# First attention of a Perceiver kernel: the projections of a superblock spread evenly over its four steps, and two evictions together in every second step

## The chip, the cores and the metric

The kernel runs on one core of a Trainium2 chip. A core has five engines that work at the same time and wait for each other by semaphores: TensorE (PE, matrix products into the accumulator memory PSUM; its weight loads are shown apart, as PEld), VectorE (DVE), ScalarE (ACT), GpSimd (POOL) and the queue that issues most transfers (SP). The metric is the time of one execution in microseconds on the device; lower is better. Of the unchanged kernel three runs are at hand: 1592.82, 1596.47 and 1597.17 us, median 1596.47.

## The reference, cut to what matters

Six sublayers are applied to one sequence x of 128 rows of 256. The change touches the first one, an attention of the 128 rows over 12544 context rows of 192, with 16 heads of 16:

```python
q = (x @ Wq + bq).reshape(B, N, NUM_HEADS, HEAD_DIM)
k = (y @ Wk + bk).reshape(B, M, NUM_HEADS, HEAD_DIM)
v = (y @ Wv + bv).reshape(B, M, NUM_HEADS, HEAD_DIM)
scores = jnp.einsum('bnhd,bmhd->bhnm', q, k) * scale
attn = jax.nn.softmax(scores, axis=-1)
out = jnp.einsum('bhnm,bmhd->bnhd', attn, v).reshape(B, N, IMAGE_DIM)
h = jax.nn.relu(out @ W1 + b1)
return h @ W2 + b2
```

Here x is layer-normalised and y is the context. Everything is float32. Behind it come a causal self-attention of the 128 rows, a dense mixture of eight experts, a second attention over the same context with 16 heads of 64, a small self-attention and a second mixture.

## The kernel before, in words

The first attention treats the 16 heads as two octets, j = 0 and 1. For each octet the 12544 context rows are walked in 13 superblocks of up to 1024 rows (`SB`), and each superblock in groups of 256 rows: four per superblock, one in the last, short superblock. That makes 49 groups per octet and 98 in all; `groups[t]` holds (superblock m, group g). The main loop over t (line 562) does one step per group, and all instructions are issued in the order in which the loop writes them (`tc.manual_schedule`), so each engine works off its own list in order.

In step t, TensorE computes the scores of group t (`scores`, line 421: 16 recorded matmuls of 256 columns) into two PSUM tiles st[0] and st[1] of two banks each. `keep` (line 434) lets ScalarE copy st[0] and then st[1] to SBUF slots (line 441), while VectorE takes a running maximum of st[1] and then of st[0] (line 447). The two engines never read one of the two tiles at the same time: the copy of st[1] waits for its maximum, and the maximum of st[0] waits for its copy. The two tiles are the only ones for scores, so the scores of the next group need both emptied.

A range is ten groups (nine in the last of an octet). The softmax of a range is shifted by its own maximum. When a range has ended, in the next step, VectorE folds the running maximum (`fold`, line 455, instructions of line 464, or of line 462 in a range of nine), TensorE transposes it, VectorE reduces it to one value per head and row (`range_maximum`, line 466), one or two steps later TensorE spreads the value over columns (`range_spread`, line 480) and ScalarE copies the spread to SBUF (line 494). Then the scores of that range, which lie in their slots, are shifted: by POOL for three quarters and by VectorE for one quarter (`shift`, line 502, instructions of line 506), 12 and 11 groups behind the scores (`LAG` = 13; VectorE one step ahead of POOL). ScalarE takes the exponents in place (line 517), and one step later TensorE multiplies them with the values (`attend`, line 519, 32 recorded matmuls, "p * v"). At the end of a range the result is collected and turned (`collected`, `gather`, lines 538 and 543).

Keys and values are projected four groups ahead (`AHEAD` = 4) by `pieces(t + 4)`, line 368. A projection of 192 context columns has two parts per half superblock r: a tiled part over the last 64 columns, in which both halves run at the same time on two halves of the array, and a whole part over the first 128, one per half (`project_keys`, line 200; `project_values`, line 216). One unit, the keys or the values of a superblock, fills two PSUM banks, one per half, and each bank is evicted by one instruction: keys with the bias (line 390), values into their place among columns of ones (line 256). In the first steps, up to t = 11, ScalarE does these evictions (`filling`), from then on VectorE. Before the change the four steps of a superblock do this (g is the group projected for): g = 0 tiled keys, whole keys of half 0, its eviction; g = 1 whole keys of half 1, its eviction; g = 2 and g = 3 the same for values. So g = 0 and g = 2 are heavy steps of TensorE and g = 1 and g = 3 light ones. The short superblock does all of it in one step.

PSUM has eight banks: four for the two score tiles, two for the projections (`ps_w`, taken in turn, and used by `range_maximum`, `range_spread` and `gather` too), one "m" for a range's spread and one "o" for p * v. The order of a step for VectorE is: maximum of st[1], maximum of st[0], a fold if a range has ended, the shift, the eviction. For TensorE: scores, a spread if one is due, the projection, p * v, then a range's maximum and the turning of a result. Where the value buffer that is to be filled is the one that p * v still reads (`same`, line 591), the projection is issued behind p * v.

## Time and profile before

| what | us |
|---|---|
| three runs | 1592.82, 1596.47, 1597.17 |
| profiled execution, its own time | 1592.66 |
| its span, first to last instruction | 1590.9 |
| PE busy in the span | 1507.9 |
| DVE busy | 1169.4 |
| ACT busy | 996.3 |
| POOL busy | 851.1 |
| first scores of the first attention start | 13.86 |
| POOL's first shift starts | 57.70 |
| last p * v of the first attention starts | 459.7 |

The first attention is thus the first 29% of the span. In the profile, a row of the timeline holds a start time, a length, the engine, the line of the program, the operation, the tiles (written <- read), their shapes and a count; rows of equal instructions that follow each other are merged into one. In brackets stands how long the engine was idle before it and what ended that. [...] Starts of consecutive instructions on one engine tell more than their lengths, since an instruction's length holds the acknowledgement of its writes, which overlaps the next one.

### The profile page before, as it was taken

How to read it: one execution, taken by the hardware profiler on the slowest of the kernel's cores; microseconds unless marked ns; L12 is line 12 of the kernel's file. 1: busy time of each engine (PE TensorE's matmuls, PEld its weight loads, DVE VectorE, ACT ScalarE, POOL GpSimd, SP SyncE). 2: the span in 40 equal slices, each digit the busy share in tenths (PEclk: the TensorE clock that was granted, in tenths of full speed). 3: DMA queues.
4: the chain of work that ended last, by engine and by line, in shares of the span. 5: the costliest groups of instructions: out<-in, count | busy, mean ns of one | idle time of the engine just before them, and what ended most of it. 6: DMA issues, size and time to landing. Idle time of an engine off the chain costs nothing.

```text
span 1590.9 us, 39751 instructions
## 1 busy us (share of the span) xinstructions
PE 1507.9 (95%) x17130; PEld 1156.8 (73%) x17130; DVE 1169.4 (74%) x1238; ACT 996.3 (63%) x1221; POOL 851.1 (54%) x559
## 2 busy tenths in 40 slices
PE   7999989999789998999999999999999999999978
PEld 4566666666545877877778787787787777777868
DVE  4798978999863327677777777777777777778952
ACT  5898979889853225665655665565665655655531
POOL 0588877888820000863863864864764764761000
PEclk9999999999997999999999999999999999999979
DMA  3211112111193661322222222232232222225930
GB/s 104 61 41 42 46 42 61 41 42 46 47 270 129 238 167 25 98 84 83 83 80 86 81 81 86 80 93 74 87 94 80 87 81 86 81 81 153 306 135 4
DMA packets 68737, 146.62 MB, mean 92 GB/s; under 512 B 8905, under 2 KB 27089, under 8 KB 68562
## 3 DMA queue, kind: packets, MB, share of 16 engines
q1 hardware_dynamic: 68258, 143.30, 30.0%
q8 instruction: 135, 2.21, 0.6%
q10 hardware_dynamic: 304, 0.79, 0.2%
q14 instruction: 40, 0.33, 0.1%
HBM read 143.92 MB, written 0.13 MB: 91 GB/s over the span
## 4 chain that ended last, share of the span: by engine, by line
PE 62%; DVE 6%; ACT 2%; POOL 1%; DMA 1%; issue 1%; SPq 0%; DVEq 0%; ACTq 0%
PE x_s L958 11%; PE x_v L234 10%; PE x_o L1043 10%; PE x_k L212 9%; PE x_v L227 5%; PE x_k L209 4%; PE f_h L1249 2%; PE f_h L824 2%; PE k L212 2%; PE f_py L841 2%; DVE x_part L1066 1%; POOL x_p L506 1%; PE k L209 1%; DVE x_folded L1005 1%; PE f_py L1258 1%
## 5 line engine op out<-in xcount | busy, mean ns | idle before, releaser
L1024 POOL TENSOR_TENSOR x_p<-x_p,x_spread 128x1024 f32<-128x1024 f32 (+1 forms) x175 | 402.6, 2324 | 165.1 <-ACT x_spread L1017 164.9
L506 POOL TENSOR_TENSOR x_p<-x_p,x_spread 128x512 f32<-128x512 f32 (+1 forms) x184 | 325.6, 1820 | 121.0 <-ACT x_spread L494 61.1
L1066 DVE TENSOR_REDUCE x_part<-x_p 128x256 f32<-128x1024 f32 (+1 forms) x175 | 329.4, 1923 | 1.6 <-ACT x_p L1032 1.6
L975 ACT COPY x_p<-x_s 128x1024 f32<-128x1024 f32 (+1 forms) x200 | 198.0, 996 | 177.7 <-DVE x_mx L982 97.9
L982 DVE TENSOR_TENSOR x_mx<-x_s,x_mx 128x1024 f32<-128x1024 f32 (+1 forms) x161 | 193.4, 1201 | 127.1 <-PE x_s L958 118.7
L1071 POOL TENSOR_TENSOR x_sums<-x_sums,x_part 128x256 f32<-128x256 f32 x161 | 118.7, 738 | 303.4 <-DVE x_part L1066 303.1
L441 ACT COPY x_p<-x_s 128x1024 f32<-128x1024 f32 x196 | 193.4, 1016 | 48.5 <-PE x_s L428 33.2
L234 PEld LDWEIGHTS x_v<-ywv_lo,x_ctx_lo 128*128 128x128 f32 x1568 | 189.3, 192 | 38.3 <-issue 36.8
L1032 ACT ACTIVATE x_p<-x_p 128x1024 f32<-128x1024 f32 (+1 forms) x200 | 197.8, 1037 | 1.4 <-DVE x_p L1024 1.3
L517 ACT ACTIVATE x_p<-x_p 128x1024 f32<-128x1024 f32 x196 | 196.3, 1062 | 0.2 <-DVE x_p L506 0.2
L1043 PE MATMUL x_o<-x_p,x_v 128*64 128x128 f32 x3136 | 193.6, 276 | 0.4
L234 PE MATMUL x_v<-ywv_lo,x_ctx_lo 128*128 128x128 f32 x1568 | 193.1, 276 | 0.0
L447 DVE TENSOR_TENSOR x_mx<-x_s,x_mx 128x1024 f32<-128x1024 f32 x140 | 168.2, 1221 | 32.1 <-PE x_s L428 17.2
L1043 PEld LDWEIGHTS x_o<-x_p,x_v 128*64 128x64 f32 x3136 | 169.6, 137 | 12.3 <-issue 1.5
L958 PE MATMUL x_s<-x_qT,x_kT 64*128 64x128 f32 x2744 | 177.7, 279 | 0.0
L212 PE MATMUL x_k<-x_ctx_lo,ywk_lo 128*128 128x512 f32 (+1 forms) x364 | 171.6, 594 | 0.0
L958 PEld LDWEIGHTS x_s<-x_qT,x_kT 64*128 64x128 f32 x2744 | 160.2, 188 | 15.6 <-issue 15.4
L943 ACT COPY x_v<-x_v 128x512 f32<-128x512 f32 (+1 forms) x208 | 116.2, 563 | 79.3 <-PE x_v L234 78.8
L227 PEld LDWEIGHTS x_v<-ywv_hi,x_ctx_hi 64*128 64x128 f32 x1568 | 106.8, 188 | 48.4 <-issue 25.1
L428 PE MATMUL x_s<-x_qz,x_kT 32*128 32x256 f32 x1568 | 117.6, 401 | 17.7 <-ACT x_p L441 16.6
L530 PE MATMUL x_o<-x_p,x_v 128*32 128x128 f32 x3136 | 111.7, 276 | 10.0 <-ACT x_p L517 8.5
L530 PEld LDWEIGHTS x_o<-x_p,x_v 128*32 128x32 f32 x3136 | 81.9, 109 | 53.9 <-ACT x_p L517 18.9
(257 smaller groups left out, 1761.1 us busy)
## 6 DMA issues: line engine op xcount, KB each, us to landing
x_ctx_lo<-in_ctxT_dram SPq DMA_DIRECT2D x119, 512.0 KB, 4.0
x_ctx_hi<-in_ctxT_dram SPq DMA_DIRECT2D x238, 128.0 KB, 3.8
f_w<-in_L_ffn_W_dram SPq DMA_DIRECT2D x32, 512.0 KB, 4.9
k_lo<-in_ctxT_dram SPq DMA_DIRECT2D x12, 512.0 KB, 10.0
f_gating<-n_kernel_gating_EDF_dram SPq DMA_DIRECT2D x8, 512.0 KB, 6.9
f_up<-L_ffn_kernel_up_EDF_dram SPq DMA_DIRECT2D x8, 512.0 KB, 7.5
f_wd<-ffn_kernel_down_EFD_dram SPq DMA_DIRECT2D x8, 512.0 KB, 7.3
k_hi<-in_ctxT_dram SPq DMA_DIRECT2D x24, 128.0 KB, 7.9
```

What stands on the lines that cost most here:

```text
L212: nc.tensor.matmul(ps[r][:, :h], wk[0][:, js], lo[:, r * h : (r + 1) * h], start=False, stop=True)
L234: nc.tensor.matmul(ps[r][:, kc * P : (kc + 1) * P], lo[:, r * h + kc * P : r * h + (kc + 1) * P], wv[0][:, js], start=False, stop=True, sk ...
L441: nc.scalar.copy(ps[t][k], st[k].rearrange("p a n -> p (a n)"))
L506: engine.tensor_tensor(v, v, by[:, banks].unsqueeze(2).to_broadcast([P, n, 2, 256]), ALU.add)
L517: nc.scalar.activation(ps[t][k], ps[t][k], AF.Exp)
L530: nc.tensor.matmul(os[b][32 * i : 32 * i + 32, u * P : (u + 1) * P], v[:, 2 * g + c, 17 * (2 * i + u) : 17 * (2 * i + u) + 32], p[i // 2][ ...
L958: nc.tensor.matmul(st[:, u, c * P : (c + 1) * P], kTs[t][rs, ks], qT[rs, j, :], start=True, stop=True)
L975: nc.scalar.copy(scores_kept(ps[t][i], sts[i].shape[2] // P), sts[i])
L1024: engine.tensor_tensor(v, v, spreads[j].unsqueeze(2).to_broadcast([P, 2, n, P]), ALU.add)
L1032: nc.scalar.activation(v, v, AF.Exp)
L1043: nc.tensor.matmul(o[us, 0:P], vs[t][:, c0 + c, us], p[:, n0 : n0 + P], start=(c0 + c == 0), stop=(c0 + c == total - 1), skip_group_check= ...
L1066: nc.vector.tensor_reduce(part, v, AX.X, ALU.add)
```

## The change

Three things change, all in the first attention.

First, the projection of a unit is cut so that each of its two steps has the same number of matmuls: the even step (g = 0 or 2) does the tiled part and the first half of the whole part of half 0; the odd step (g = 1 or 3) does the second half of it, evicts bank 0, does the whole part of half 1 and evicts bank 1. For keys this cuts each 512-column matmul into two of 256 columns (`of=2`). Both banks stay taken from the even step to the end of the odd one. Where another use of these two banks falls into the even step (`shared`: a range has just ended, a result is turned, or a spread is due in the next step), the pair of steps keeps the old division. The short superblock stays in one step.

Second, in an odd step the projection with its evictions is issued ahead of VectorE's shift (`evicting`); in an even step the shift stays ahead.

Third, the first steps are cut accordingly: the keys of the first superblock start before the loop with the tiled part and all of the whole part of half 0, in two halves, and the rest follows in step 0. The test `same` now looks at the last group alone (and the short superblock), since the values of an unfinished unit are written in the last step.

```diff
--- before.py
+++ after.py
@@ -197,23 +197,32 @@
             )
         return lo, hi, h
 
-    def project_keys(name, wk, cx, j, bank=None):
+    def project_keys(name, wk, cx, j, bank=None, of=1):
 
         lo, hi, h = cx
         ps = [(bank or ps_w)(f"{name}_{r}") for r in range(2)]
         js = slice(j * P, (j + 1) * P)
 
         def tiled():
-            for r in range(2):
-                rs = slice(64 * r, 64 * r + 64)
-                nc.tensor.matmul(ps[r][:, :h], wk[1][rs, js], hi[rs, :h], start=True, stop=False)
-
-        def whole(r):
-            nc.tensor.matmul(ps[r][:, :h], wk[0][:, js], lo[:, r * h : (r + 1) * h], start=False, stop=True)
+            for i in range(of):
+                n = slice(i * h // of, (i + 1) * h // of)
+                for r in range(2):
+                    rs = slice(64 * r, 64 * r + 64)
+                    nc.tensor.matmul(
+                        ps[r][:, n], wk[1][rs, js], hi[rs, n], start=(i == 0), stop=False, skip_group_check=True
+                    )
+
+        def whole(r, parts=range(of)):
+            for i in parts:
+                n = h // of
+                nc.tensor.matmul(
+                    ps[r][:, i * n : (i + 1) * n], wk[0][:, js], lo[:, r * h + i * n : r * h + (i + 1) * n],
+                    start=False, stop=True, skip_group_check=True,
+                )
 
         return ps, tiled, whole
 
-    def project_values(name, wv, cx, j, bank=None):
+    def project_values(name, wv, cx, j, bank=None, of=1):
 
         lo, hi, h = cx
         ps = [(bank or ps_w)(f"{name}_{r}") for r in range(2)]
@@ -229,8 +238,9 @@
                         skip_group_check=True,
                     )
 
-        def whole(r):
-            for kc in range(h // P):
+        def whole(r, parts=range(of)):
+            n = h // P // of
+            for kc in range(parts.start * n, parts.stop * n):
                 nc.tensor.matmul(
                     ps[r][:, kc * P : (kc + 1) * P], lo[:, r * h + kc * P : r * h + (kc + 1) * P],
                     wv[0][:, js], start=False, stop=True, skip_group_check=True,
@@ -361,9 +371,16 @@
 
                 return bank_o(name) if name.endswith("_1") else bank_m(name)
 
+
+            spread_at = {max(l + 2, l0 + LAG - 2): b for b, (l0, l) in enumerate(zip(start_of, last_of))}
+
+            def shared(t):
+
+                return t > 0 and (last[t - 1] or (t > LAG and last[t - LAG - 1]) or t + 1 in spread_at)
+
             def behind(t):
 
-                return ((1, 2), (3, 4), (5, 6), (7,))[t] if t < 4 else (t + AHEAD,)
+                return ((2,), (3, 4), (5, 6), (7,))[t] if t < 4 else (t + AHEAD,)
 
             def pieces(t):
 
@@ -377,8 +394,6 @@
                 lo, hi, h = ctxs[m]
                 v = vs[m % NV]
                 bias = cols[:, COL_BK + j : COL_BK + j + 1]
-                work_of = {"k": ([], [], []), "v": ([], [], [])}
-
 
                 filling = t < LAG - 1 + AHEAD
 
@@ -394,29 +409,38 @@
                     dst = v[:, r * n : (r + 1) * n, 0:136].rearrange("p k (h d) -> p k h d", d=17)[:, :, :, 0:16]
                     evacuated(filling, dst, src[:, :h].rearrange("p (k h d) -> p k h d", h=8, d=16))
 
-                def first_half(kind, make, w, evacuate):
+                def unit(kind):
+                    if kind == "k":
+                        make, w, out = project_keys, xwk, keys_out
+                    else:
+                        make, w, out = project_values, xwv, values_out
                     bank = spare if kind == "v" and m < 2 else None
-                    unit = make(f"x0_{kind}{m}", w, ctxs[m], j, bank)
-                    tiled, whole, out = work_of[kind]
-                    tiled.append(unit[1])
-                    whole.append(lambda: unit[2](0))
-                    out.append(lambda: evacuate(0, unit[0][0]))
-                    deferred[m, kind] = lambda: unit[2](1), lambda: evacuate(1, unit[0][1])
+                    return make(f"x0_{kind}{m}", w, ctxs[m], j, bank, 1 if s == NS - 1 else 2), out
+
+
+
+
+                def first_half(kind):
+                    (banks, tiled, whole), out = deferred[m, kind] = unit(kind)
+                    if shared(t - AHEAD):
+                        return [tiled, lambda: whole(0), lambda: out(0, banks[0])]
+                    return [tiled, lambda: whole(0, range(0, 1))]
 
                 def second_half(kind):
-                    for part, f in zip(work_of[kind][1:], deferred.pop((m, kind))):
-                        part.append(f)
-
-                short = s == NS - 1
-                if g == 0:
-                    first_half("k", project_keys, xwk, keys_out)
-                if g == 1 or short:
-                    second_half("k")
-                if g == 2 or short:
-                    first_half("v", project_values, xwv, values_out)
-                if g == 3 or short:
-                    second_half("v")
-                return [f for kind in "kv" for part in work_of[kind] for f in part]
+                    (banks, tiled, whole), out = deferred.pop((m, kind))
+                    rest = [lambda: whole(0, range(1, 2)), lambda: out(0, banks[0])]
+                    return (rest if not shared(t - 1 - AHEAD) else []) + [lambda: whole(1), lambda: out(1, banks[1])]
+
+                if s == NS - 1:
+                    both = [unit(kind) for kind in "kv"]
+                    return [
+                        f for (banks, tiled, whole), out in both for f in (
+                            tiled, lambda whole=whole: whole(0), lambda whole=whole: whole(1),
+                            lambda out=out, banks=banks: out(0, banks[0]),
+                            lambda out=out, banks=banks: out(1, banks[1]),
+                        )
+                    ]
+                return (first_half, second_half)[g % 2]("kv"[g // 2])
 
             def scores(t):
                 m, g = groups[t]
@@ -549,16 +573,14 @@
                 )
 
             with tc.manual_schedule():
-                tiled, whole, k_out = pieces(0)
-                tiled()
-                whole()
+                (tiled, lo0), (lo1, k_out, *left) = pieces(0), pieces(1)
+                for f in (tiled, lo0, lo1):
+                    f()
                 early = ps_s("x0_early")
                 _, xnT = layernorm(x, "ln0", early[:, 0])
                 k_out()
                 queries(0, xnT, early[:, 1])
                 oTs = {}
-
-                spread_at = {max(l + 2, l0 + LAG - 2): b for b, (l0, l) in enumerate(zip(start_of, last_of))}
                 for t in range(len(groups) + LAG + 1):
                     e, o = t - LAG + 1, t - LAG
                     e = e if 0 <= e < len(groups) else None
@@ -580,17 +602,21 @@
                             exponent(e, k)
                     if ended is not None:
                         fold(ended)
-                    if 0 <= t - LAG + 2 < len(groups) and not first[t - LAG + 2]:
+
+                    evicting = t + AHEAD < len(groups) and groups[t + AHEAD][1] % 2
+                    if not evicting and 0 <= t - LAG + 2 < len(groups) and not first[t - LAG + 2]:
                         shifted_vector(t - LAG + 2)
-                    ahead = [f for n in behind(t) for f in pieces(n)]
+                    ahead = left + [f for n in behind(t) for f in pieces(n)]
+                    left = []
 
                     same = False
                     if o is not None and ahead:
                         (m, g), (mo, go) = groups[t + AHEAD], groups[o]
-                        short = sbs[m][1] == NS - 1
-                        same = m % NV == mo % NV and (short or g == 3 or (g == 2 and go < 2))
+                        same = m % NV == mo % NV and (g == 3 or sbs[m][1] == NS - 1)
                     for f in () if same else ahead:
                         f()
+                    if evicting and 0 <= t - LAG + 2 < len(groups) and not first[t - LAG + 2]:
+                        shifted_vector(t - LAG + 2)
                     if o is not None:
                         attend(o)
                         if last[o]:
```

## The prediction

> **What bounds the kernel now.** The change touches only the first attention, so I read the page for engine shares, then the timeline of POOL alone over that attention, then all engines over two steps, then VectorE at the end of a range. The page names no single bound: PE is busy 95% of the span, and in the stretch 57.70 to 186.56 PE, VectorE, ScalarE and POOL are busy 121.3, 116.0, 117.0 and 107.3 of 128.9 us. What sets the pace has to be found in the order of events.
>
> First POOL's timeline. POOL adds the negated maxima to a range of ten groups, and one merged row is one range (20 instructions).
>
> ```profile
> 186.56 35.74 POOL L506 TENSOR_TENSOR x_p<-x_p,x_spread 128x1024 f32<-128x1024 f32 x20 [7.24 <-DVE x_mx L447]
> 231.45 32.16 POOL L506 TENSOR_TENSOR x_p<-x_p,x_spread 128x1024 f32<-128x1024 f32 x18 [9.14 <-DVE x_mx L447]
> 273.21 35.77 POOL L506 TENSOR_TENSOR x_p<-x_p,x_spread 128x1024 f32<-128x1024 f32 x20 [9.60 <-DVE x_mx L447]
> 316.21 35.74 POOL L506 TENSOR_TENSOR x_p<-x_p,x_spread 128x1024 f32<-128x1024 f32 x20 [7.24 <-DVE x_mx L447]
> 359.14 35.74 POOL L506 TENSOR_TENSOR x_p<-x_p,x_spread 128x1024 f32<-128x1024 f32 x20 [7.18 <-DVE x_mx L447]
> ```
>
> Columns are start, length, and in brackets the idle time before. POOL runs its 35.75 us without a stop, and the next range starts 7.2 us after it ends: at 100.61, 143.56, 186.56, 316.21, 359.14 and 402.12. Only at 231.45 and 273.21 (around the change of octet) is the gap longer. A gap that repeats to 0.06 us means that POOL's end itself starts the chain to the next range. VectorE's timeline at the end of a range shows how:
>
> ```profile
> 305.54 0.68 DVE L506 TENSOR_TENSOR x_p<-x_p,x_m 128x512 f32<-128x512 f32 x1
> 306.13 0.68 DVE L256 COPY x_v<-x_v 128x512 f32<-128x512 f32 x1
> 306.73 3.40 DVE L464 TENSOR_TENSOR x_spread<-x_mx 128x512 f32<-128x512 f32 x2
> 310.05 0.68 DVE L506 TENSOR_TENSOR x_p<-x_p,x_m 128x512 f32<-128x512 f32 x1
> 310.65 0.74 DVE L390 TENSOR_SCALAR x_kT<-x_k,cols 128x512 f32<-128x512 f32 x1
> ```
>
> The fold (L464, two instructions that read and write SBUF only) takes 3.40 us; where POOL was already idle, at 264.68, its instructions took 0.68 each. POOL ended at 273.21 + 35.77 = 308.98; the first fold instruction ended at 309.53, 0.55 later. The folds at 91.53, 134.05, 177.08, 349.61 and 392.66 likewise end 0.55 after POOL's last instruction, though they were issued 1.9 to 2.35 us before it. So in these six ranges the fold waits for POOL, and everything up to the next range (shift, eviction, PE's transposes, the scores, ScalarE's copy of the spread) hangs on it: 7.2 us. From one POOL start to the next is 43.0 us, whatever the steps between do, as long as the fold is issued before POOL ends.
>
> Third, a light and a heavy step in the middle of a range:
>
> ```profile
> 293.93 1.15 PE L428 MATMUL x_s<-x_qz,x_kT 32*128 32x256 f32 x16
> 295.17 1.01 ACT L441 COPY x_p<-x_s 128x1024 f32<-128x1024 f32 x1
> 295.17 2.36 DVE L447 TENSOR_TENSOR x_mx<-x_s,x_mx 128x1024 f32<-128x1024 f32 x2 [0.32 <-PE x_s L428]
> 296.49 1.01 ACT L441 COPY x_p<-x_s 128x1024 f32<-128x1024 f32 x1 [0.30 <-DVE x_mx L447]
> 297.39 2.01 ACT L517 ACTIVATE x_p<-x_p 128x1024 f32<-128x1024 f32 x2
> 297.55 1.16 PE L428 MATMUL x_s<-x_qz,x_kT 32*128 32x256 f32 x16 [0.41 <-ACT x_p L441]
> 299.30 1.92 ACT L441 COPY x_p<-x_s 128x1024 f32<-128x1024 f32 x2
> 300.34 1.23 DVE L447 TENSOR_TENSOR x_mx<-x_s,x_mx 128x1024 f32<-128x1024 f32 x1 [0.32 <-ACT x_p L441]
> 301.48 0.68 DVE L506 TENSOR_TENSOR x_p<-x_p,x_m 128x512 f32<-128x512 f32 x1
> 302.02 1.15 PE L428 MATMUL x_s<-x_qz,x_kT 32*128 32x256 f32 x16
> ```
>
> The light step (one whole projection) lasts 3.62: scores to maximum 1.24, maximum to ScalarE's second copy 1.32, that copy 1.01, and PE, which waited 0.41, goes on 0.05 later. The heavy step is PE's own work: 4.47 here, 4.34 in the keys' step before. Four steps are 4.34 + 3.62 + 4.47 + 3.62 = 16.05.
>
> **The change part by part.** *Even split.* PE's work is not reduced. Keys are now issued in 256 columns, 8 rows where there were 4 for the tiled part, and as many again for the whole part: 16 more rows and as many loads per superblock. No row shows that width for keys; eight 128-column values rows take 1.07 (299.92 to 300.99 before p * v at 301.01) and two 512-column keys rows 1.05 (291.87 to 292.92), so smaller pieces cost between 0 and 0.02 per projection. I take 0.02. Half a whole projection, 0.53, moves from the even to the odd step. PE then needs 1.08 + 1.06 + 0.53 + 1.02 = 3.69 in an even step (1.06: tiled keys at 30.98 to 32.04, without a wait) and 1.08 + 0.53 + 1.05 + 1.02 = 3.68 in an odd one: about 3.7 in both, 3.72 for values.
>
> *Both evictions in the odd step, ahead of the shift.* ScalarE's work stays (2 copies 0.90 each, 296.49 to 297.39; 2 exponents 1.91, 297.39 to 299.30). VectorE's also stays per pair, but an odd step now holds two maxima, two evictions and the shift, 2 x 1.14 + 2 x 0.66 + 0.60 = 4.2, in a step that wants 3.7. Queued behind the shift is the next step's maximum, behind that (0.09 after its end) ScalarE's second copy, behind that the exponents and the next copy, on which VectorE's second maximum waits. This loop runs through one pair of steps: maximum to second copy 1.32; to the exponents 0.90; to the next copy 1.91; to the maximum that waits for it 1.04 (299.30 to 300.34); to the next VectorE instruction 1.14 (300.34 to 301.48); two evictions 2 x 0.66 for keys (281.78 to 282.44) or 2 x 0.60 for values (306.13 to 306.73); the shift 0.60. Sum 8.23 for keys and 8.11 for values, against 7.96 and 8.09 now. So a split pair costs +0.27 and +0.02, on average **+0.14**, and PE, with 7.4 of work, is no longer what sets a pair. The cover for PE's extra rows is this loop; without it they would cost 0.02 each.
>
> *Banks.* A unit holds both projection banks until its second eviction. In an odd step of the loop ScalarE is still at the exponents until about 1.75 after the scores; the waiting maximum starts 1.04 later at 2.8 and ends at 4.05 with the step, and the evictions run from 3.9 to 5.3 (keys) or 5.2. The next tiled matmuls are wanted at 4.05 + 1.08 = 5.13. The wait is 0.1 to 0.2, as today (tiled keys take 1.19 at 290.68 and 1.06 without a wait), and PE has 0.3 to spare: 0. The Trainium skill, "Perfetto Trace Analysis", section "Matmuls", asks that independent matmul groups rotate through PSUM banks so that one's evacuation overlaps the next's matmuls, which speaks against holding both. By that rule PE would see one whole eviction, 0.66, per pair, some 5 us over the seven pairs that count below; by the rows it sees 0.2, under cover.
>
> *Steps that keep the old split.* Where a range's maximum, spread or gather needs those banks, the pair is as before: 3 of 16 pairs up to the first short block (20, 30, 40) and 6 of 24 after it (49, 53, 59, 69, 79, 89). 13 + 18 = 31 pairs are split. All the folds lie in unsplit steps, so the 7.2 us from POOL's end to the next range, with its shift, eviction and waits, is untouched. The context loads stay in the step of group 0; the SP and POOL queues have no instruction moved.
>
> *What of this reaches the end.* In a range paced by POOL, four split pairs (0.56) and VectorE's late shift put the fold back. That shift ends 5.7 after its step's scores in a step of 4.05, so 1.67 into the next one, where the fold now starts at 1.09 (306.73 - 305.64): 0.58. Together 1.1, against 1.9 to 2.35 us that the fold now waits. It is hidden: **0** for six ranges; the fold's wait just gets shorter. The Trainium skill, "SBUF — State Buffer", section "Who interferes with whom", says that a VectorE instruction with two SBUF inputs is blocked by a GpSimd one that reads SBUF until that one finishes. The trace agrees that it blocks, but at 307.75 one POOL instruction ended and the fold went on waiting to 308.98, the last. By the rule as by the row, a fold issued 1.1 later falls into POOL's last instruction and ends where it does now.
>
> Not covered are three stretches. 186.56 to 273.21 holds six split pairs (0.84) and two folds that find no POOL to wait for (0.58 each); against it the short block's step and the step of the spread, where VectorE idles 0.99 and 2.48, take back what is late, about 0.4 each: +1.2. 402.12 to 439.14: one split pair and the short block: +0.2. 0 to 57.70: evictions are on ScalarE, a pair lasts 6.33 (41.74 to 48.08), PE's work in it is 2 x 1.08 + 3.2 = 5.4. At best 0.9 comes off three pairs, -2.8; at worst the two evictions of 0.7 in one step delay the copies by one, +2.1. PE's even halves speak for the lower half; I take -0.4.
>
> Sum: 0 + 1.2 + 0.2 - 0.4 = **+1.0 us**. The profiled execution took 1592.66 (span 1590.9), so 1593.7 by its own time; it lies 3.8 below the median of the three runs, and I carry the difference to the median: 1596.47 + 1.0 = 1597.5.
>
> **The rivals.** *The fold outlives its cover (slower).* The point is exact: when a pair costs more than (2.25 - 0.58) / 4 = 0.42, the fold is issued after POOL has ended. For it: 0.14 rests on intervals of 0.1 us, and a wait of PE for both banks that isn't under cover adds to it. At 0.7 a pair, fold and pairs overrun by 1.1 in six ranges, 6.7 us, the seven uncovered pairs add 4.9 and two folds 1.2: +13, 1609. Just past the point it is 7 x 0.42 + 1.2 = +4, 1601.
>
> *POOL does not pace the ranges (slower).* If the fold waits on something that moves with the steps, all counts: 31 x 0.14 + 8 x 0.58 = +9, 1605. Against it: six ends at 0.55 after POOL, and gaps of 7.2 to 0.06.
>
> *The split does what balance could do (faster).* If VectorE's surplus slipped under ScalarE, a pair would fall to ScalarE's 7.4 or PE's 7.4, -0.6. But a gain is swallowed by POOL's 35.75 + 7.2 too; only the uncovered stretches keep it: 7 x -0.6 - 2.8 = -7.0 at the most, 1589.5; half of it is likelier.
>
> **How the numbers follow.** The likeliest case, hidden by POOL, gets 0.70, its own range 1593 to 1601. The fold past its cover 0.12 and no pacing 0.09 (together 1601 to 1609), the gain 0.09. A difference of 0.3% is 4.8 us, and the three runs of before lie 4.4 apart. Slower by more: most of the two slower rivals, 0.19; faster by more 0.07; same 0.74. The range that leaves out less than 2 in 10 is 1591 to 1605.
>
> **What would show it.** In the new profile: pairs of about 4.05 + 4.1 in place of 4.35 + 3.62; two L390 or L256 rows back to back in every second step, and ScalarE's second copy waiting about 0.7 for the maximum in even steps; POOL's rows still 35.75 long with 7.2 between; the fold's two instructions together down from 3.4 to some 2.3. I am wrong if POOL's gaps are wider than 7.2 in the six ranges (rival one), if the fold no longer ends 0.55 after POOL (rival two), or if the stretch 186.56 to 273.21 is shorter than 86.65 by more than 2.

## The result and the profile after

The changed kernel takes 1596.86 us (median of 12 runs, 1592.86 to 1601.65), the kernel before 1595.76 beside it (12 runs, 1590.98 to 1600.27): a ratio of 1.0011, interval 0.9996 to 1.0026. A second set of runs gave 1.0016 (1.0005 to 1.0026). So the change makes no difference of 0.3%; if anything it costs one or two microseconds. The profiled execution took 1597.11 with a span of 1595.4, where before it was 1592.66 and 1590.9. This gap of 4.5 us is larger than that of the medians, and it is not the change that made most of it, as the experiments show.

POOL's timeline of the changed kernel, around the change of octet (start, length, count, and in brackets the idle time before):

```profile
188.38 35.71 POOL L530 TENSOR_TENSOR x_p<-x_p,x_spread 128x1024 f32<-128x1024 f32 x20 [7.24 <-DVE x_mx L471]
234.32 32.15 POOL L530 TENSOR_TENSOR x_p<-x_p,x_spread 128x1024 f32<-128x1024 f32 x18 [10.24 <-DVE x_mx L471]
277.45 35.76 POOL L530 TENSOR_TENSOR x_p<-x_p,x_spread 128x1024 f32<-128x1024 f32 x20 [10.97 <-DVE x_mx L471]
320.44 35.76 POOL L530 TENSOR_TENSOR x_p<-x_p,x_spread 128x1024 f32<-128x1024 f32 x20 [7.24 <-DVE x_mx L471]
363.38 35.74 POOL L530 TENSOR_TENSOR x_p<-x_p,x_spread 128x1024 f32<-128x1024 f32 x20 [7.18 <-DVE x_mx L471]
```

Ranges of ten groups still last 35.75 and the gaps of 7.2 are as they were, to 0.02 us. Of these rows only the two around the octet change have a longer gap (9.14 and 9.60 before). On the page TensorE is busy 95% of the span as before, with 192 rows more and 9.8 us more busy time; neither tells where the time went. VectorE's timeline at the end of the range that starts at 277.45 shows what was hidden:

```profile
310.29 1.28 DVE L266 COPY x_v<-x_v 128x512 f32<-128x512 f32 x2
311.48 0.68 DVE L530 TENSOR_TENSOR x_p<-x_p,x_m 128x512 f32<-128x512 f32 x1
312.08 2.28 DVE L488 TENSOR_TENSOR x_spread<-x_mx 128x512 f32<-128x512 f32 x2
314.28 0.67 DVE L530 TENSOR_TENSOR x_p<-x_p,x_m 128x512 f32<-128x512 f32 x1
314.88 0.74 DVE L405 TENSOR_SCALAR x_kT<-x_k,cols 128x512 f32<-128x512 f32 x1
```

Both evictions stand together ahead of the shift, and the fold (L488) is issued 1.12 ahead of POOL's end at 313.20 where it was 2.23 ahead. It takes 2.28 in place of 3.40 and its first half ends 0.55 after POOL, as before. In all six paced ranges the fold comes 0.84 to 1.13 ahead of POOL's end, where it came 1.89 to 2.35 ahead. The lateness has been paid out of the fold's wait. A split pair, from the timeline of all engines of the changed kernel:

```profile
336.78 1.41 PE L452 MATMUL x_s<-x_qz,x_kT 32*128 32x256 f32 x16
336.92 1.40 DVE L405 TENSOR_SCALAR x_kT<-x_k,cols 128x512 f32<-128x512 f32 x2
338.12 1.41 PE L236 MATMUL x_v<-xwv_hi,x_ctx_hi 64*128 64x128 f32 x16
338.24 0.68 DVE L530 TENSOR_TENSOR x_p<-x_p,x_m 128x512 f32<-128x512 f32 x1
338.83 2.35 DVE L471 TENSOR_TENSOR x_mx<-x_s,x_mx 128x1024 f32<-128x1024 f32 x2
340.14 1.01 ACT L465 COPY x_p<-x_s 128x1024 f32<-128x1024 f32 x1 [0.61 <-DVE x_mx L471]
341.21 1.16 PE L452 MATMUL x_s<-x_qz,x_kT 32*128 32x256 f32 x16
342.30 1.60 PE L244 MATMUL x_v<-xwv_lo,x_ctx_lo 128*128 128x128 f32 x12
344.92 0.92 PE L452 MATMUL x_s<-x_qz,x_kT 32*128 32x256 f32 x8
```

From scores to scores the even step lasts 4.43 and the odd one 3.71. Inside the even step TensorE waits where the rows are longer than their work: scores 1.41 for 1.15, tiled 1.41 for 1.07 (both evictions end about 338.3). ScalarE's second copy waits 0.61 for the maximum behind the shift and ends at 341.15, when TensorE too is at the end of its own rows (341.19), so these rows don't say which of the two sets the step. Split pairs mostly take 8.09 (keys) and 8.21 (values), before 7.96 and 8.09.

### The profile page after: what moved, and what is told of

Same layout as the page of the kernel before. It is cut to its first block, busy times and chain, and to the rows that moved or that the text cites. A ratio compares the mean times of both kernels' runs of the same rounds, so it can differ in the third digit from the quotient of the medians.

```text
span 1595.4 us, 40149 instructions
## 1 busy us (share of the span) xinstructions
PE 1517.7 (95%) x17322; PEld 1194.7 (75%) x17322; DVE 1161.8 (73%) x1238; ACT 994.0 (62%) x1221; POOL 853.1 (53%) x559
## 4 chain that ended last, share of the span: by engine, by line
PE 63%; DVE 5%; ACT 2%; DMA 1%; issue 1%; POOL 0%; SPq 0%; DVEq 0%; ACTq 0%
PE x_s L984 11%; PE x_v L244 11%; PE x_o L1069 10%; PE x_k L218 9%; PE x_v L236 5%; PE x_k L211 4%; PE f_h L1275 2%; PE f_h L850 2%; PE f_py L867 2%; PE k L218 2%; DVE x_part L1092 1%; DVE x_folded L1031 1%; PE k L211 1%; PE f_py L1284 1%; DMA x_ctx_hi<-in_ctxT_dram 1%
## 5 line engine op out<-in xcount | busy, mean ns | idle before, releaser
L452 PE MATMUL x_s<-x_qz,x_kT 32*128 32x256 f32 x1568 | 124.6, 403 | 9.7 <-ACT x_p L465 7.6
L955 ACT COPY x_kT<-x_k 128x512 f32<-128x512 f32 (+1 forms) x91 | 50.9, 559 | 109.9 <-PE x_k L218 109.9
```

## Experiments

Theory: in six of the ranges POOL's end paces the kernel, because the fold waits for it, and a split pair's small loss (VectorE has too much in the odd step) is hidden there; what is left comes from the stretches that POOL does not cover. Rivals: POOL paces nothing and the steps simply cost little; or TensorE's smaller pieces are what costs.

### The change once more, and the hold taken away

The first run repeats the changed kernel. In the next two the fold uses its other form, a reduction with a single input, in all ranges: first in the kernel before, then in the changed one. The result stays the same.

```diff
-                    if last_of[b] - start_of[b] < 9:
+                    if last_of[b] - start_of[b] < 10:
                         nc.vector.tensor_reduce(dst, m.rearrange("p a c n -> p a n c"), AX.X, ALU.max)
```

> The changed kernel, unaltered, profiled a second time. In the first profile it started POOL 1.86 us later than the kernel before (59.56 against 57.70) and lost another 2.4 around the change of octet (188.38 to 277.45 takes 89.07 against 86.65) and 1.07 at the end (406.37 to 444.46 takes 38.09 against 37.02). In all three places TensorE's rows took up to twice their usual time for 2 to 4 us (scores 2.09 in place of 1.15 at 15.06; p * v 1.65 at 236.95 and 1.91 at 441.22 in place of 1.08). Theory A, that these slow stretches fall by chance: here they lie elsewhere or are missing, and where one is missing the stretch is shorter by 0.6 to 3. Theory B, that the new order of matmuls brings them about: they lie at the same three places. Either way the six gaps of POOL stay 7.2.

> The kernel before, with every fold of a range made by the reduction that the ranges of nine groups use (1.25 us each, and not held up at 217.81, where POOL was busy), in place of the two-input maximum. If the fold's wait for POOL paces the ranges: from the fold's issue to the next VectorE instruction it takes 2.3 (217.81 to 220.10) in place of 3.0 to 3.5, so POOL's six gaps fall from 7.2 to about 6.2 (6.5 in the first), some -5.7 us; the two folds that POOL did not hold up (50.45 and 264.68) get 1.1 slower each; together -3.5, 0.998. If the fold only moves with the steps and its length is its own: two reductions of 1.25 in place of 3.4 is the same -1 per range, but the changed kernel with the same edit must then gain as much.

> The changed kernel with the same edit of the fold. If POOL paces the ranges, the changed kernel has already used the fold's wait up to 0.95 to 1.12 us (fold at 312.08, POOL's end at 313.20): from issue to the next instruction 2.2 to 2.3 before and 2.3 after the edit, so POOL's six gaps stay near 7.2 and the two other folds cost 1.1 each: 0 to +2 us against the changed kernel. The kernel before with the edit is then 5 to 8 us faster than this one, where without the edit the two differ by 1 to 2: the loss that was hidden comes into view. If the hidden loss is a fiction, both kernels change by the same amount.

The repeat: ratio 1.0016, span 1594.5, and POOL's starts within 0.13 us of the first profile. The slow stretches lie at the same places (granted clock 0.50 from 234.78 and from 439.58), as its theory B, the new order of matmuls, wanted it; what settled this against theory B stands further below. Before with the reduce: 1587.73, ratio 0.9953 (0.9938 to 0.9968). The changed kernel with the reduce: 1599.06, ratio 1.0026 (1.0012 to 1.0040). POOL's timeline of the kernel before with the reduce:

```profile
272.53 35.75 POOL L506 TENSOR_TENSOR x_p<-x_p,x_spread 128x1024 f32<-128x1024 f32 x20 [9.60 <-DVE x_mx L447]
314.52 35.71 POOL L506 TENSOR_TENSOR x_p<-x_p,x_spread 128x1024 f32<-128x1024 f32 x20 [6.24 <-DVE x_mx L447]
```

and VectorE's timeline in the range's end between them:

```profile
306.05 2.38 DVE L462 TENSOR_REDUCE x_spread<-x_mx 128x512 f32<-128x1024 f32 x2
308.34 0.68 DVE L506 TENSOR_TENSOR x_p<-x_p,x_m 128x512 f32<-128x512 f32 x1
```

POOL ended at 308.28 and the reduction at 308.43, so it ran its 1.2 per instruction while POOL was busy: it isn't held. The gap falls to 6.24, and the six gaps together by 5.6 us (the first by 0.65, the others by 1.0), which the interval of the ratio (5 to 10 us) holds. This is the hold that both kernels pay, and taking it away from the kernel before beats both. In the two ranges where nothing held the fold the slower form cost nothing: from the fold's issue to POOL's next start it takes 7.25 (from 50.45 before, from 52.44 here) and 8.53 (from 264.68 and from 264.00) in both kernels. I had charged 1.1 for each.

With the reduce the changed kernel is 11.3 us slower than the kernel before with the reduce, while without it the two differ by 2.1. The six gaps alone are 6.9 of it: 7.35 to 7.65 in the changed kernel, where the other has 6.21 to 6.54. The same range's row in POOL's timeline of the changed kernel with the reduce:

```profile
323.24 35.78 POOL L530 TENSOR_TENSOR x_p<-x_p,x_spread 128x1024 f32<-128x1024 f32 x20 [7.36 <-DVE x_mx L471]
```

So the change does cost time in these ranges, and the hold hides it. The rival without pacing falls: it wants the same difference in both. Most of the rest lies around the octet change (90.90 against 86.64), where the clock dropped twice in the changed kernel's profile (203.84 and 237.98) and not once in the other's, so it can't all be put down to the change.

### A little more work in each split pair

A part of the second eviction (64 columns) is repeated in every split pair behind the fill; the values written are the same.

```diff
+                def once_more(kind, src):
+                    w, n = 64, h // P
+                    if kind == "k":
+                        nc.vector.tensor_scalar(kTs[m][:, h : h + w], src[:, :w], bias, None, ALU.add)
...
-                    return (rest if not shared(t - 1 - AHEAD) else []) + [lambda: whole(1), lambda: out(1, banks[1])]
+                    again = [] if filling or shared(t - 1 - AHEAD) else [lambda: once_more(kind, banks[1])]
+                    return (rest if not shared(t - 1 - AHEAD) else []) + [lambda: whole(1), lambda: out(1, banks[1])] + again
```

> The changed kernel, in which VectorE evicts the first 64 columns of the second bank once more in each odd step of a split pair (the same result; about 0.19 us by the slope of the rows of 128 and 512 columns). Theory: a split pair grows by 0.19, four pairs take 0.76 of the 0.95 to 1.12 us by which the fold is still issued ahead of POOL's end, so the six gaps of POOL stay 7.2; only the uncovered stretches grow, by about 1.5 us in all against the changed kernel. Rival, no pacing by POOL: 31 x 0.19 and 0.19 per fold, +7 us. Rival, VectorE isn't in the loop that sets a pair: pairs stay 8.1 to 8.2.

It cost 7.6 us against the changed kernel, not 1.5: 1604.87, ratio 1.0062 (1.0045 to 1.0079). The extra row puts VectorE's shift back by 0.27 behind values (1.46 from the first eviction, 315.10 to 316.56, where the changed kernel takes 1.19, 310.29 to 311.48) and by 0.32 behind keys. Pairs got 0.26 (keys) to 0.32 (values) longer, as much as VectorE's queue; the rival that VectorE isn't in the loop of a pair falls. The fold now reaches POOL's end almost exactly (0.22 after to 0.16 ahead of it), and POOL's six gaps are 7.74 to 8.07. The number is the rival's, but not its mechanism: four pairs are some 1.2 longer, and of this only 0.5 to 0.9 came out in a gap, so part of it is still hidden. POOL's timeline shows the next gap:

```profile
325.05 35.75 POOL L541 TENSOR_TENSOR x_p<-x_p,x_spread 128x1024 f32<-128x1024 f32 x20 [7.74 <-DVE x_mx L482]
```

What came late is TensorE. Its timeline ahead of this gap with the extra work, where POOL ended at 317.31:

```profile
314.89 1.48 PE L463 MATMUL x_s<-x_qz,x_kT 32*128 32x256 f32 x16
316.30 1.54 PE L211 MATMUL x_k<-x_ctx_hi,xwk_hi 64*128 64x256 f32 x8
317.77 1.13 PE L218 MATMUL x_k<-x_ctx_lo,xwk_lo 128*128 128x256 f32 x4
318.83 1.08 PE L565 MATMUL x_o<-x_p,x_v 128*32 128x128 f32 x32
319.84 1.09 PE L509 MATMUL x_mt<-ident,x_spread 128*128 128x128 f32 x8
```

And in the changed kernel, where POOL ended at 313.20:

```profile
313.74 1.08 PE L554 MATMUL x_o<-x_p,x_v 128*32 128x128 f32 x32
315.01 1.32 PE L498 MATMUL x_mt<-ident,x_spread 128*128 128x128 f32 x8 [0.19 <-DVE x_p L530]
```

In the kernel before, where POOL ended at 308.98:

```profile
310.78 1.32 PE L474 MATMUL x_mt<-ident,x_spread 128*128 128x128 f32 x8 [0.72 <-DVE x_p L506]
```

The fold's second half ends 1.15 after POOL in all three. But the transposes (L474, L498, L509) stand behind p * v on TensorE. Before the change they wait 0.37 to 0.77 for VectorE in the six ranges, in the changed kernel 0.00 to 0.19; with the extra work p * v, which starts 1.52 after POOL's end and not 0.54, is what they follow, and they start 2.53 after POOL's end in place of 1.81. So when POOL's hold ends, TensorE of the changed kernel has at most 0.2 us in hand, and in three of the six ranges next to nothing, although the fold still has 0.8 to 1.1. The step at a range's end says the same: 6.39 before, 5.37 with the hold taken away; 6.18 in the changed kernel, 5.97 once TensorE sets it.

### The parts of the change, one undone at a time

Undone first: TensorE's even split; both evictions stay in the odd step, and keys are still issued in 256 columns. Second: the order of eviction and shift.

```diff
-                    return [tiled, lambda: whole(0, range(0, 1))]
+                    return [tiled, lambda: whole(0)]
...
-                    rest = [lambda: whole(0, range(1, 2)), lambda: out(0, banks[0])]
+                    rest = [lambda: out(0, banks[0])]
...
```

> The changed kernel with TensorE's even split undone: tiled and the whole of half 0 in the even step, the whole of half 1 in the odd one, as before; both evictions stay together in the odd step, ahead of the shift. Keys are still issued in 256 columns. Theory A (the pair is set by VectorE's surplus in the odd step, the loop through two maxima, two evictions and the shift): pairs stay at 8.09 (keys) and 8.21 (values) within 0.05, now as about 4.4 + 3.7; the fold is issued 0.8 to 1.1 us ahead of POOL's end as in the changed kernel; six gaps of 7.2; ratio 1.001. Rival (TensorE's smaller pieces set the pair): pairs fall back to 7.96 and 8.09, the fold comes 0.5 earlier, 1.3 to 1.6 ahead of POOL's end, and the octet change loses 0.8 us; ratio 1.000.

```diff
-                    evicting = t + AHEAD < len(groups) and groups[t + AHEAD][1] % 2
+                    evicting = False
```

> The changed kernel with one part undone: VectorE's shift ahead of the evictions in every step, as before; TensorE's even split and both evictions in one step stay. Theory A (VectorE's surplus sets the pair; the order moves only the bank's release): the same loop, 8.09 and 8.21, but each bank comes free 0.6 later, so that the tiled matmuls of the next pair wait 0.7 to 0.8 in place of 0.1 to 0.2; TensorE has 0.3 to spare, so a pair costs 0.3 to 0.5 more. The shift no longer runs 0.6 late into the fold's step, so the fold comes 0.6 - 4 x 0.4 = 1.0 later, about at POOL's end, and the six gaps grow to 7.3 to 7.6: 2 us there, 3 in the seven uncovered pairs, +5 against the changed kernel, ratio 1.004. Rival (order does not matter, it is the same work): pairs as in the changed kernel, the fold 0.6 earlier (1.6 ahead of POOL's end), gaps 7.2, ratio 1.001.

Without the even split: 1599.23, ratio 1.0018 (1.0005 to 1.0031). Keys took 8.02 and values 8.26 a pair, on average 8.14 as in the changed kernel (8.15) and not 8.03 as before; the fold came 0.80 to 0.96 ahead of POOL's end, the six gaps stayed at 7.18 to 7.24. Each kind is off by a little more than the 0.05 I allowed, in opposite directions, but on average the loss stays when TensorE's work is put back. What is left of the change in this run is the two evictions in one step, with both banks held until then, and the loss goes with them. The rival of the smaller pieces falls for values, which are issued in the same 128 columns in all three kernels and still lose 0.12 and 0.17; for keys no run undoes the 256 columns, but with them kept keys are only 0.06 slower here than before.

With the shift first: 1603.79, ratio 1.0046 (1.0029 to 1.0063), as the theory had it. Pairs took mostly 8.14 to 8.46 (keys) and 8.30 to 8.56 (values), the fold came 0.06 to 0.66 ahead of POOL's end, and the gaps grew to 7.76 to 8.42, more than the 7.6 that I allowed. From POOL's timeline of this kernel:

```profile
325.80 35.74 POOL L530 TENSOR_TENSOR x_p<-x_p,x_spread 128x1024 f32<-128x1024 f32 x20 [8.12 <-DVE x_mx L471]
369.77 35.74 POOL L530 TENSOR_TENSOR x_p<-x_p,x_spread 128x1024 f32<-128x1024 f32 x20 [8.23 <-DVE x_mx L471]
```

The step at the range's end lasts 5.97 here too, so the gaps again go by TensorE. The eviction ahead of the shift is what keeps the change harmless: without it the two evictions in one step cost about 5 us more.

### Why the two profiles lie 4.5 us apart

POOL's gap that starts at 266.47 is 1.4 longer than before, and after TensorE's wait at 232.7 TensorE's rows are half as fast. The windows of the two profiles (stretch, its length, TensorE's busy time, count, granted clock, DMA share, GB/s). Before:

```profile
226.74:230.15 3.41, 2.67 (x29) 1.00 0.00 0
230.15:233.57 3.42, 2.20 (x26) 1.00 0.01 2
```

The changed kernel:

```profile
231.35:234.76 3.41, 1.86 (x18) 1.00 0.00 0
234.76:238.17 3.41, 3.41 (x38) 0.50 0.01 2
```

The clock falls to 0.50 for 3.41 us. The six drops of the first 640 us start at 234.76, 439.56, 466.86, 497.58, 586.33 and 634.11; the last five lie 60, 68, 77, 103 and 117 times 3.413 after the first: a fixed grid. The one at 497.58 lasts two intervals, 6.83 us. In both kernels TensorE waits 1.55 us for the copy of the spread in this step. In the profile before, a border of the grid (230.15) cuts the wait (229.81 to 231.37) in two; in the changed kernel it lies inside one interval. Two runs ask whether this is the change or chance: the kernel before in one more execution, and the changed kernel with that wait filled.

```diff
         def tiled():
+            for _ in range(9 if name == "x0_v14" else 0):
+                nc.tensor.matmul(
+                    ps[0][:, :P], lo[:, :P], wv[0][:, js], start=True, stop=False, skip_group_check=True
+                )
             for kc in range(h // P):
```

> The kernel before, unchanged, in one more profiled execution. In the four profiles of the changed kernel and its variants TensorE ran at a granted clock of 0.50 for 3.41 us once after the octet change (234.76 to 238.17 in the changed kernel), and the places of these drops within one profile are whole multiples of 3.413 us apart; in the profiles of before and of before with the reduce there was none at that place. Theory A (a matter of where a fixed grid of 3.41 us falls on TensorE's 1.55 us wait): the grid's offset against the program can differ in this execution, and the stretch from the start of the fifth range to that of the seventh lasts 86.65 if the wait is cut by a border of the grid, and about 87.8 if it lies inside one interval. Theory B (the change itself): 86.65 and no drop, wherever the grid lies; a wait inside one interval without a drop would speak for B. In both, six gaps of 7.2 us on POOL.

> The changed kernel with nine more matmuls (128 x 128, overwritten by what follows) in the step of the octet change, where TensorE waits 1.55 us for ScalarE's copy of the spread. Its result is the same. Theory A (the octet change is 2.4 us longer because TensorE's clock drops after that wait): the filled wait shrinks to about 0.3, no drop follows at 234 to 239, p * v after it takes 1.08 and not 1.65, and the stretch from the start of POOL's fifth range (188.38) to that of its seventh falls from 89.07 to between 87.6 and 88.1. Theory B (the steps themselves are longer by the split): 89.0 or, if the nine matmuls delay what follows, more. The gaps of 7.2 and POOL's 35.7 stay. On the median 0 to -1.5 us against the changed kernel, at the limit of what three rounds tell.

The kernel before, in the other execution, had the drop. Windows and POOL's timeline:

```profile
233.31:236.72 3.41, 1.86 (x21) 1.00 0.00 0
236.72:240.13 3.41, 3.41 (x34) 0.50 0.01 2
```

```profile
235.84 32.13 POOL L506 TENSOR_TENSOR x_p<-x_p,x_spread 128x1024 f32<-128x1024 f32 x18 [9.13 <-DVE x_mx L447]
279.15 21.47 POOL L506 TENSOR_TENSOR x_p<-x_p,x_spread 128x1024 f32<-128x1024 f32 x12 [11.18 <-DVE x_mx L447]
```

The wait lies inside one interval there, and the gap is 11.18, not 9.60: the stretch from 190.98 to 279.15 lasts 88.17 in place of 86.65. (It runs from the fourth range's start to the sixth's; the expectations count one too many.) The changed kernel with the wait filled, windows and POOL's timeline (the last row of this timeline, as of the one above, is cut off by the end of the view):

```profile
231.57:234.98 3.41, 3.41 (x35) 1.00 0.00 0
234.98:238.39 3.41, 3.41 (x69) 1.00 0.03 7
```

```profile
276.10 25.04 POOL L534 TENSOR_TENSOR x_p<-x_p,x_spread 128x1024 f32<-128x1024 f32 x14 [9.42 <-DVE x_mx L475]
```

No drop, a gap of 9.42, and the stretch (from 188.59) is 87.51 in place of 89.07. One kernel lost 1.5 us by the drop, the other won 1.6 by its absence: theory A holds. The other profiles without added matmuls agree: in all seven in which the wait lies inside one interval (six of them of the changed kernel and its variants) a drop follows, and in the two in which a border cuts it (before, and before with the reduce) none does. In the repeat of the changed kernel the grid lay within 0.02 us of where it lay in the first profile, hence the same places. How often each kernel meets the drop was not counted. On the median the filled kernel could not be told from the changed one or from before (1597.80, ratio 1.0001, 0.9982 to 1.0021). What remains of the change here is 87.51 - 86.65 = 0.9 us.

### Both kernels with the waits filled, and the best version

The start differs by the clock too: POOL's first range begins at 57.70 and 62.12 in the two profiles of the kernel before, and its first step lasts 4.31 and 7.26; in the second, TensorE's rows take up to twice their time there (scores 2.09 for 1.15). Twenty matmuls are added while the inputs land, beside the nine above, in the kernel before, in the changed one, and in the one before with the reduce. A last run takes 14 in place of 20.

```diff
         def tiled():
+            for _ in range(20 if name == "x0_k0" else 0):
+                nc.tensor.matmul(ps[0][:, :P], ident, ident, start=True, stop=True)
```

> The kernel before with matmuls added at two places where TensorE idles (all overwritten by what follows, the result is the same): 20 of ident x ident before the first projection, while the inputs still land, and nine in the step of the octet change. Theory A (the clock of TensorE, on its fixed grid of 3.41 us, makes the differences between profiles of the same kernel): TensorE is at full pace from the first projection on, the first tiled and whole matmuls take half of the 2.55 and 2.07 us that they took, POOL's first range starts at about 55.5 (57.70, 59.69 and 62.12 in profiles without the matmuls), and the stretch from the fifth range's start to the seventh's is 86.6 with no drop in it. On the median -3 us (2.0 that every execution gains, and what the late ones gain on top), ratio 0.998. Theory B (start and octet change vary for another reason, the inputs' landing above all): the first range still starts at 57.7 to 59.7, ratio 1.000.

> The changed kernel with the same two groups of matmuls. It asks what the change itself costs once these two clock effects are out. Theory A (the sum over the steps of the profiles without drops: -1.1 in the fill, 0 in the six ranges, +0.9 at the octet change, +0.5 at the end): within 1 us of the kernel before with the same matmuls, ratio 0.998 against the kernel before; POOL's first range at about 54.4, the stretch at the octet change 87.5. Theory B (the change costs what the medians said, 1 to 2.5 us): 1.5 to 3 above the kernel before with the matmuls, ratio 0.999 to 1.000.

> The kernel before with the reduce in every fold (as in the run that gave 0.9953) and the same two groups of matmuls. If the two gains lie in different stretches (six gaps of 7.2 on one side, start and octet change on the other) they add: 7.5 + 3 = 10.5 us, ratio 0.9934; gaps of 6.2 on POOL, first range at about 55.5. If the fill or the octet change takes back what the matmuls give: ratio 0.995.

> As the run before it (the kernel before with the reduce and both groups of matmuls), but 14 of ident x ident in place of 20. With 20 the first projection began at 8.62, 7.86 and 9.13, up to 2 us after the inputs had landed (6.59 and 7.07 in the profiles without them); 14 at the cold pace of 0.36 each end at 1.53 + 5.0 = 6.6. Theory A (that overrun took back what the full pace gave): the first projection begins at 6.6 to 7.1, POOL's first range at about 55.5, or 57.5 if the clock drops once more in the wait for the queries (11 to 13); with gaps of 6.2 the median is 1584 to 1586, ratio 0.9935. Rival (the idle time before the inputs matters little, since the copies and the queries are waited for in any case): first range at 57.5 to 59.5, ratio 0.995.

The kernel before, filled: 1589.97, ratio 0.9976 (0.9962 to 0.9990). TensorE's timeline at its start (one matmul is recorded as two rows, so the twenty show as x40):

```profile
1.53 7.17 PE L208 MATMUL x_k<-ident 128*128 128x128 f32 x40 [1.53 <-POOL headmask L93]
8.62 1.13 PE L211 MATMUL x_k<-x_ctx_hi,xwk_hi 64*128 64x512 f32 x4
9.68 1.12 PE L214 MATMUL x_k<-x_ctx_lo,xwk_lo 128*128 128x512 f32 x2
```

The first projections take 1.13 and 1.12, not 2.55 and 2.07, but twenty were too many: the inputs were there at about 7, and POOL's first range starts at 57.16, not 55.5. That is 0.5 us earlier than in the first profile of before and 5.0 earlier than in the second; how much of the median's 4.5 us comes from the start is not shown. The changed kernel, filled: 1590.24, ratio 0.9969 (0.9956 to 0.9983), first range at 55.01, octet stretch 87.52. The two medians lie 0.3 us apart, so theory A (within 1 us) is favoured, but intervals of 2 us to either side do not exclude theory B.

With the reduce and twenty matmuls nothing came on top: 1587.58, ratio 0.9949 (0.9932 to 0.9967); the first projection began at 9.13, and the clock fell again (0.50 from 14.54). With 14 matmuls the first projection begins at 6.69, POOL's first range at 56.05, and the time is 1587.05, later than the 55.5 and 1584 to 1586 expected; the ratio of 0.9936 (0.9916 to 0.9956) is the lowest of all. That it beats the reduce alone (0.9953) is likely from the traces but not shown by these intervals.

## Why the prediction was right, point by point

Predicted were 1597.5 and no measurable difference; measured were 1596.86 and a ratio of 1.0011. The mechanism, a hold that hides the cost, was right. That the predicted +1.0 us stands so close to the +1.1 between the medians is in part luck: the terms were off in both directions, and the interval of the ratio runs from -0.6 to +4.1 us. The sum can be checked stretch by stretch. "Clock" is what drops, the cold start and the inputs' landing made of the difference between the two first profiles.

| stretch | predicted | measured | clock | the change's own |
|---|---|---|---|---|
| start to POOL's first range | -0.4 | +1.9 | +2.9 | -1.1 |
| six paced ranges | 0 | 0.0 | | 0.0 |
| fourth to sixth range's start | +1.2 | +2.4 | +1.5 | +0.9 |
| ninth to tenth range's start | +0.2 | +1.1 | +0.6 | +0.5 |
| sum | +1.0 | +5.3 | +5.0 | +0.3 |

At the start, the second step's scores begin at 21.11 where they began at 18.17, +2.9; without the change they began at 20.16 (with the reduce) and 22.59 (in the other execution of before), so it need not be the change. From there to POOL's first range the changed kernel gains 1.1 (38.45 where it took 39.53). In the two filled kernels its first step is 0.4 shorter too (3.87 against 4.31), so its own part of the start may be -1.5 and the sum about 0. At the end, the steps ahead of the drop at 439.56 take 22.31 where they took 21.82, +0.5; the other 0.6 falls in the drop.

**POOL's end paces six ranges, so 0.** Right, and shown: the gaps are unchanged in both profiles of the changed kernel, and the cost is visible when the hold is gone. One argument for it was too strong: that the gaps repeat to 0.06 us doesn't show that POOL's end starts the chain, since without the hold five of the six repeat to 0.03 as well (6.21 to 6.24). The fold's end at 0.55 after POOL and the run with the reduce show it.

**A split pair costs 0.14.** Right on average (0.13 and 0.12), wrong in its parts: +0.27 and +0.02 were predicted, and steps of 4.05 + 4.1 where 4.4 + 3.7 came. What was wrong is the loop, which put the delay into the odd step's end and the banks' wait of 0.1 to 0.2 under cover. The delay came in the even step, where the tiled matmuls wait about 0.3 for the banks. That VectorE's surplus is the cause is supported by the extra work, which lengthened pairs by as much as VectorE's queue; but it held the second bank longer too, and no run separates the surplus from the banks' late release.

**The fold is put back 1.1, against 1.9 to 2.35.** Right: its lead fell by 0.9 to 1.4, from between 1.89 and 2.35 to between 0.84 and 1.13.

**The rival's point, 0.42 a pair.** Wrong. At 0.42 (0.13 and 0.29 by the extra work) the fold reached POOL's end as worked out, but the gaps had by then grown by 0.5 to 0.9. I took the fold's wait for the whole cover. What TensorE had in hand ahead of its transposes was 0.4 to 0.8 a range before and 0.0 to 0.2 after, so by an estimate from these waits the point lies between 0.13 and 0.17 a pair, and the prediction was closer to the slower rival than its chance of 0.12 says.

**The octet change, +1.2.** Right in size (0.9) by other terms: one pair (steps 47 and 48) lost 0.76, since the projection that stands behind p * v there has now 12 rows (1.60) where it had 8 (1.16), and the p * v ahead of it waits 0.39 for ScalarE; the next pair, 49 and 50, lost 0.2; the other steps gave a little back. The 1.5 by the clock had no term.

**The fill, -0.4, and the end, +0.2.** Both mis-sized, in opposite directions: -1.1 (or -1.5), within the bounds given, and +0.5.

The profile of before lies 3.8 below its median, and I carried that difference over as it was. Part of it is now known: that execution had no drop around the octet change, which cost 1.5 in the other one.

What stays open: the sum over the steps is +0.3 us or a little less, the medians say +1.1 to +2.1. Later drops, which differ from execution to execution (from POOL's last start to the end of the span it takes 1149 to 1152 in twelve of fourteen profiles, 1146 and 1155 in the others), may make the rest; this was not settled.

## What to carry to other kernels

When a hold hides a loss, look for everything that waits on the hold's end and take the smallest lead among them, not the lead of the one instruction that is held. A loss under cover is still a loss: taking the cover away (here a reduction with one input in place of a maximum of two) gained 0.5% for the kernel before and laid bare 7 us of the change's cost in six gaps where there had been none. Before a difference of a few microseconds between two profiles is put down to the code, read the granted clock in windows: the spans of the kernel before differed by 6.8 us between its two profiles, 4.4 of it at the start and 1.5 around the octet change.

## What the hardware showed

The granted TensorE clock falls to 0.50 for one interval of 3.41 us or several in a row (two at 497.58 in the changed kernel), on a grid of 3.413 us that is fixed within an execution and lies differently against the program in another: the wait for the spread began 0.34 ahead of a border in one profile of before and 0.90 behind one in the other. A wait of 1.55 us was enough when it lay inside one interval (TensorE busy 0.54 or 0.55 of it, seven profiles of seven), and did nothing when a border cut it (0.78 and 0.64 in one profile, 0.77 and 0.78 in the other). The Trainium skill, "TensorE: Matmul & The Clock Gate", section "Part 1: The HAM clock gate", gives the same window, 3413 ns, as free-running, and the traces agree. The page lets the clock fall after an idle window of about 3.4 us; here less than half a window of idle time did it, and the measurement decides. Busy time in the profile does not tell when the clock falls either: an interval with 0.66 busy was followed by a drop (463.45 in the changed kernel), one with 0.54 was not (431.54 in the kernel before), so what is counted stays open.

A VectorE maximum with two SBUF inputs waited for POOL's run of instructions to end: in the first profiles of both kernels all twelve folds that were issued ahead of POOL's end finished their first instruction 0.55 after it. A reduction with one input ran at its usual 1.2 per instruction beside POOL.
